# A fused cross-attention and quantised feed-forward kernel: the maximum of h over partitions, the first group's parts, the run-ahead of gelu and p, and the engine of the weights' middle part D

## Chip, cores and metric

One core of a Trainium2 chip runs the whole kernel. The metric is the device time of one execution in microseconds, as a median of several runs. One further execution is recorded by the hardware profiler; all rows of profile below come from such a recording. The engines are called PE (TensorE, the matrix engine), DVE (VectorE), ACT (ScalarE), POOL (GpSimd) and SP (SyncE, which issues most DMAs).

## What is computed

Input x has 2 x 2048 rows of 512. The reference, cut to what matters:

```python
x = x + xattn(layernorm(x), ctx)             # 128 keys per batch, softmax over them
h = layernorm(x)
h = act_qdq(h)                               # 16 bits, one scale: max|h| over the whole tensor
up   = act_qdq(h @ lpbq_dequant(w_up).T)     # 512 -> 1536
gate = act_qdq(h @ lpbq_dequant(w_gate).T)   # 512 -> 1536
sig  = fixed_qdq_u16(sigmoid(gate))
gate = act_qdq(gate * sig)
o    = act_qdq(gate * up)
x = x + o @ lpbq_dequant(w_down).T           # 1536 -> 512
```

`act_qdq` divides by max|x|/32767, rounds, clips and multiplies back; `lpbq_dequant` rounds the weights to 4 bits with a scale for each block of 32. Each `act_qdq` needs the maximum over a whole tensor before the next product can begin, so the program falls into stages.

## The kernel before

The 4,096 rows are 8 groups of 512 (`NG`, `TG`), kept with features on the partitions. A product is made of integers: a 16-bit integer n is split into a = n/4096 rounded, n − 4096a, and 4097a − n, three `parts` in fp32r; a weight is split likewise into H (its high bits), D (weight − H), and a third part made from H and the weight. A "projection" is 12 matmuls of 128x512: 8 into a sum q (parts 0 and 1), then 4 into a sum e (third parts); the value is q·(1 + 1/4096) − e.

The stages, by the profiled execution's span:

- **Prologue, 0 to 177 us.** For each group: `front` (transposes of x, L295; row statistics), `scores` (L314), `turn` (transposes of e into PSUM, then the copy eT on ACT, L419), `attend` (po, L431; x + po, L432), `normalise` (square with row sums on ACT, L449; inverse root on POOL, L284; h on ACT, L460), the maximum of |h| into a column of `hmax` (`abs_max`, L169), and `lift` (transposes of h, L471, copied to hT by ACT, L472). Between them runs `split_weights` for w_gate in four portions of 384 rows, as a generator that is advanced a step at a time: load L175, block maxima L169, scale L181 and L183, integers L185, dequantised L187, transposes L193, copy by ACT L194, then on DVE H (L196), D (L198) and the third part (L201), then the store. The group after the last does its rows one by one.
- **Maximum of h.** `over_partitions` reduces `hmax` to one column on DVE (m_h, L140) and over the partitions on POOL (a_h, L142). `act_scale` makes the scale s_h (L151) and its reciprocal r_h. The integers hi of group 0 are rounded by DVE in four chunks (L542), those of the others in whole, the odd groups by DVE (L549), the even ones by ACT (L551). `split_integers` makes the parts: sa (L235), cast on ACT (L236), then L237 and L238 on DVE.
- **Gate stage, 177 to 455 us.** For each group t and each of three sets k of four weight chunks (n = 3t + k): four projections (L528 for q, L532 for e); g by ACT (L579) and DVE (L580); one step of the preparation of w_up and then w_down (`advance`, again `split_weights`, four portions each); then the maximum of the four (gmax, L169) and a store. PSUM holds three q and three e.
- **Up stage, 455 to 720 us.** 24 tiles in 48 half-tiles c, groups in reverse order: two projections, u by ACT (L726) and DVE (L727), stored to `up_d`; `next_gelu` (three ACT passes over a stored gate tile, L624 to L626) once per tile and once more at c = 1 and c = 13; `integers_of_p` once per tile (L661, DVE), stored to `p_d` (L662); `bound` (|u| on ACT, L669; largest product with p, L670) for a bound of max|o|. In the tile (t, k) = (0, 0), whose half-tiles are c = 42 and 43, the first parts of w_down are loaded (L699), four chunks at the start of it and four at its end.
- **Junction, 720 to 734.5 us.** `fetch_best` takes the best entries of the bound (L676 to L680, giving `row`) and gathers the u and p of those rows by indirect DMA from `up_d` and `p_d` (L685). The maximum of u over the partitions goes through PE: m_u (L765), a transpose of m_u broadcast to 128 columns (L767), and a reduction of the result (L769). ACT rounds u (ui_b, L784), DVE takes the largest products (L786), POOL reduces them over the partitions (L791), DVE makes a_o and a flag; `scale_of_o` (six small DVE operations, L909 to L914) follows, and a branch reads the flag (L926). The branch's body is not run here.
- **Down stage, 734.5 us to the end.** For each 128 rows: oi and its parts (L859 to L866), 36 matmuls (yq L874, ye L882), q scaled by ACT (L887), x added by POOL (L889), e by DVE (L893), store.

Each engine works through its instructions in order. The order of the instructions of one engine comes from a scheduler, which is held in places by `in_order` (an order without a wait). Tiles of a pool are reused after `bufs` further tiles, and wait for the release.

Of the kernel before, what the change touches and what calls it, by code (L numbers as in the profile page):

```python
# [63 lines left out]
P = 128  # L64
# [12 lines left out]
def tile_xattn_ffn(  # L77
# [66 lines left out]

    def act_scale(a, name, unit=None):


        if unit is not None:
            nc.vector.tensor_scalar(a, a, unit, None, ALU.mult)
        s = const.tile([P, 1], F32, name=f"s_{name}")  # L150
        nc.vector.tensor_scalar(s, a, 1.0 / QMAX, TINY, ALU.mult, ALU.max)  # L151
        r = const.tile([P, 1], F32, name=f"r_{name}")
        nc.vector.reciprocal(r, s)
        if unit is not None:
            nc.vector.tensor_scalar(r, r, unit, None, ALU.mult)
        return s, r
# [14 lines left out]
    def split_weights(pool, psum, src, dst, name):  # L171
# [26 lines left out]
        nc.vector.tensor_tensor(ws[:, 1], ws[:, 2], ws[:, 0], ALU.subtract)  # L198
# [58 lines left out]
    with ExitStack() as c0:  # L257

        with ExitStack() as c1:
# [153 lines left out]
            def turn(g, e):  # L413
# [5 lines left out]
                nc.scalar.copy(eT, pe)  # L419
# [86 lines left out]
            lift(NG - 1, hs.pop(NG - 1))  # L506

# [15 lines left out]
        def project(w, parts, q, e):  # L523


            for c in range(ND):
                for s in range(2):
                    nc.tensor.matmul(  # L528
                        q, lhsT=w[:, s, c, :], rhs=parts[:, s, c, :], start=(c + s == 0), stop=(c + s == ND)
                    )  # L530
            for c in range(ND):
                nc.tensor.matmul(e, lhsT=w[:, 2, c, :], rhs=parts[:, 2, c, :], start=(c == 0), stop=(c == ND - 1))  # L532

        with ExitStack() as c2:
            wg = [load_parts(wg_d, f, "wg") for f in range(NF)]
            s_h, r_h = act_scale(*over_partitions(hmax, name="h"), "h")
# [4 lines left out]
            for c in range(ND):  # L541
                nc.vector.tensor_scalar(hi[0][:, c], hT[:, c, :TG], r_h, QMAX, ALU.mult, ALU.min)  # L542
            first = split_integers(wk1, homes[0], hi[0], [ND, TG], "g0", ND)

            table = const.tile([P, 1], F32, name="table")
            nc.scalar.activation(table, unit, AF.Sigmoid)
            for t in range(1, NG):
                if t % 2:
                    nc.vector.tensor_scalar(hi[t], hT[:, :, ts(t, TG)], r_h, QMAX, ALU.mult, ALU.min)  # L549
                else:  # L550
                    nc.scalar.activation(hi[t], hT[:, :, ts(t, TG)], AF.Copy, scale=r_h)  # L551
            hpool.__exit__(None, None, None)
            home1 = tc.tile_pool(name="parts1", bufs=1, side="right")
            homes.append(ctx.enter_context(home1))
            wk2 = c2.enter_context(tc.tile_pool(name="wkb2", bufs=2))
            wpp = c2.enter_context(tc.tile_pool(name="wprep", bufs=1))
# [3 lines left out]
            steps = chain(split_rows(wpp, ps_t, w_up, wu_d, "u"), split_down(wpp, ps_t))  # L560
            groups, wu = {}, []
            for t in range(NG):
# [8 lines left out]
                for k in range(NK):  # L571
                    n = t * NK + k
                    g4 = wk2.tile([P, NQ, TG], F32, tag="g4", name=f"g4_{n}")
                    for i in range(NQ):
                        m = NQ * n + i
                        q = ps_m.tile([P, TG], F32, tag="q", name=f"q_g{m}")
                        e = ps_m.tile([P, TG], F32, tag="e", name=f"e_g{m}")
                        project(wg[NQ * k + i], parts, q, e)
                        nc.scalar.activation(g4[:, i, :], q, AF.Copy, scale=1.0 + 1.0 / BASE)  # L579
                        nc.vector.tensor_tensor_reduce(  # L580
                            g4[:, i, :], g4[:, i, :], e, 1.0, LOWEST, ALU.subtract, ALU.max, gtop[:, m : m + 1]
                        )
                        advance(steps, 1)
# [13 lines left out]
    with ExitStack() as c3:  # L597
# [50 lines left out]
        wd, ready = [], []  # L648
# [9 lines left out]
        def integers_of_p(j):  # L658
            gi, sq = ready[j]
            pi = kept_p[j % NK]  # L660
            nc.vector.scalar_tensor_tensor(pi, gi, k_p, sq, ALU.mult, ALU.mult)  # L661
# [3 lines left out]
            return pi  # L665
# [36 lines left out]
        LAST = len(order) - 1  # L702
        for j, (t, k) in enumerate(order):
# [11 lines left out]
            if j:  # L715
                pi = integers_of_p(j)
            for h in range(2):
# [12 lines left out]
                else:  # L730
                    for i in range(2):
# [6 lines left out]
                        abs_max(umax[:, LAST + 1 + i : LAST + 2 + i], v)  # L738
                stored = nc.sync.dma_start(out=up_d[c], in_=u4[:, both, :])
                if h == 0:  # L740
                    next_gelu()
                if c == 0:
                    pi = integers_of_p(0)

                if c in (1, NH // 4 + 1):
                    next_gelu()
# [10 lines left out]
            if t == 0 and k == 0:  # L757
                load_down(range(NE, NE + NQ), slice(0, 2))
# [5 lines left out]
        m_u = const.tile([P, 1], F32, name="m_u")  # L764
        nc.vector.tensor_reduce(m_u, umax, AX.X, ALU.max)  # L765
        rows = ps_m.tile([P, 2, TG], F32, tag="q", name="rows_u")[:, 0, :P]
        nc.tensor.transpose(rows, m_u.to_broadcast([P, P]), ident)  # L767
        a_u = const.tile([P, 1], F32, name="a_u")
        nc.vector.tensor_reduce(a_u, rows, AX.X, ALU.max)  # L769
# [24 lines left out]
    with ExitStack() as c5:  # L794
# [112 lines left out]
        def scale_of_o(a_o):  # L907

            nc.vector.tensor_scalar(k_o, a_o, 1.0 / QMAX, tiny_o, ALU.mult, ALU.max)  # L909
            nc.vector.reciprocal(k_o, k_o)  # L910
            nc.vector.tensor_tensor(s_o, a_o, s_pu, ALU.mult)
# [4 lines left out]
        uis = {0: up_integers(0)}  # L916
        in_order(rounded[0], *round_up(uis[0], 0, 0, P))
        scale_of_pu()
        a_o = const.tile([P, 1], F32, name="a_o")
# [4 lines left out]
        scale_of_o(a_o)  # L924
        known = nc.values_load(flag[0:1, 0:1], min_val=0, max_val=1)
        with tc.If(known == 0):  # L926
            with tc.tile_pool(name="gen", bufs=1) as gp:
# [37 lines left out]
                a, = over_partitions(omax, name="om")  # L965
                for k in range(NK):
# [6 lines left out]
                scale_of_o(a)  # L973
# [7 lines left out]
        for m in range((last + 1) * NU + 2):  # L981
# [4 lines left out]
            if m <= last * NU + NU - 1:  # L986
# [27 lines left out]
                if m == 0:  # L1014
                    in_order(casts[-1], *round_up(ui, 0, P, P))
# [32 lines left out]
```

## Time and profile before

| | us |
|---|---|
| median of 3 runs (1004.01 to 1007.13) | 1007.1 |
| profiled execution | 1005.54 |
| its span | 1003.7 |
| PE busy in the span | 942.7 (94%) |
| DVE busy | 810.7 (81%) |
| ACT busy | 548.3 (55%) |
| POOL busy | 89.6 (9%) |
| mean granted TensorE clock | 0.976 |

The profile of one execution has a page (busy time per engine; 40 equal slices of the span, each digit the busy share in tenths, PEclk the granted TensorE clock in tenths; DMA queues; the chain of work that ended last; the costliest groups) and a trace that can be asked for stretches and single instructions. In a timeline row come start, duration, engine, line of the kernel, operation, output and inputs with shapes; "[5.06 <-ACT parts_g L236]" says that the engine had been idle for 5.06 us before and what released it; "issue" is idle time in which it waited for nothing that the profile shows. PEld is the weight load of PE, which overlaps the matmuls. Busy time is an average over stages with different limits: what an edit is worth is read from its own stage.

### The profile page before, as it was taken

What the parts mean: (1) busy time and instruction counts of PE and PEld (TensorE: products, weight loads), DVE (VectorE), ACT (ScalarE), POOL (GpSimd) and SP (SyncE); (2) the same over time, 40 slices, a digit from 0 to 9 for tenths busy, and PEclk for the clock granted to TensorE, in tenths of its full rate; (3) what the DMA queues carried; (4) which work ended last, traced back from release to release, by engine and by line L of the source; (5) the groups of instructions that cost most, each with busy time, mean ns of one, the idle gap of its engine ahead of it and who ended that gap; (6) DMA issues with size and microseconds to landing.
All of it is one profiled execution on the core that took longest, in us unless ns stands there. A gap on an engine that the chain in (4) does not pass through costs nothing. (4 is left out here: it accounts for less than half of the span.)

```text
span 1003.7 us, 11683 instructions
## 1 busy us (share of the span) xinstructions
PE 942.7 (94%) x4321; PEld 762.9 (76%) x4321; DVE 810.7 (81%) x1000; ACT 548.3 (55%) x652; POOL 89.6 (9%) x67
## 2 busy tenths in 40 slices
PE   6997884999999999999999999999779999999998
PEld 5765652788888878887788788888557888888886
DVE  4579874999998989645899789887889999888882
ACT  2277786532333223226998998897454445444331
POOL 0101111000000000000000000000011232222221
PEclk9999896999999999999999999999879999999999
DMA  9177652987886666698899798988885676755611
GB/s 345 32 304 283 220 220 79 401 313 303 330 355 248 265 210 210 224 353 328 306 363 375 258 366 328 378 320 328 288 311 215 206 269 222 250 190 160 245 66 43
DMA packets 103596, 263.72 MB, mean 263 GB/s; under 512 B 6064, under 2 KB 46000, under 8 KB 94832
## 3 DMA queue, kind: packets, MB, share of 16 engines
q1 hardware_dynamic: 102496, 259.02, 69.4%
q0 software_dynamic: 512, 2.88, 0.8%
q10 hardware_dynamic: 528, 1.05, 0.3%
q8 instruction: 34, 0.56, 0.2%
q14 instruction: 26, 0.21, 0.1%
HBM read 136.05 MB, written 126.88 MB: 262 GB/s over the span
## 5 line engine op out<-in xcount | busy, mean ns | idle before, releaser
L528 PE MATMUL q_g<-parts_g,wg 128*128 128x512 f32 x768 | 195.0, 394 | 5.1 <-ACT parts_g L236 5.1
L528 PEld LDWEIGHTS q_g<-parts_g,wg 128*128 128x128 f32 x768 | 143.5, 189 | 35.4 <-ACT parts_g L236 5.8
L579 ACT ACTIVATE g<-q_g 128x512 f32<-128x512 f32 x96 | 57.3, 599 | 169.6 <-PE q_g L528 158.9
L528 PE MATMUL q_u<-parts_u,wu 128*128 128x512 f32 x576 | 142.4, 390 | 0.6 <-ACT u L726 0.6
L528 PEld LDWEIGHTS q_u<-parts_u,wu 128*128 128x128 f32 x576 | 108.1, 188 | 23.3 <-ACT u L726 1.0
L874 PE MATMUL yq<-wd,o_parts 128*128 128x512 f32 x512 | 122.1, 391 | 0.0
L874 PEld LDWEIGHTS yq<-wd,o_parts 128*128 128x128 f32 x512 | 96.9, 189 | 20.3
L532 PE MATMUL e_g<-parts_g,wg 128*128 128x512 f32 x384 | 104.0, 392 | 0.1
L580 DVE CUSTOM_DVE_ANT_0 g<-g,e_g 128x512 f32<-128x512 f32 x96 | 64.4, 681 | 37.2 <-PE e_g L532 37.0
L532 PEld LDWEIGHTS e_g<-parts_g,wg 128*128 128x128 f32 x384 | 72.3, 189 | 15.6 <-DVE parts_g L238 0.5
L889 POOL TENSOR_TENSOR qx<-yqs,x 128x512 f32<-128x512 f32 x32 | 63.7, 1991 | 204.3 <-ACT yqs L887 167.9
L874 PE MATMUL yq<-first_wd,o_parts 128*128 128x512 f32 x256 | 65.5, 399 | 13.2 <-ACT o_parts L863 13.2
L887 ACT ACTIVATE yqs<-yq,q_o 128x512 f32<-128x512 f32 x32 | 22.0, 686 | 101.8 <-PE yq L874 101.8
L532 PE MATMUL e_u<-parts_u,wu 128*128 128x512 f32 x288 | 77.1, 390 | 0.0
L866 DVE SCALAR_TENSOR_TENSOR o_parts<-sa,oi 128x1536 fp32r<-128x1536 int16 (+2 forms) x41 | 62.8, 1548 | 15.6 <-PE ye L882 15.6
L863 ACT CAST o_parts<-sa 128x1536 fp32r<-128x1536 int16 (+2 forms) x41 | 48.6, 1189 | 43.9 <-DVE sa L860 43.9
L670 DVE CUSTOM_DVE_ANT_0 ua<-ua,pi 128x1024 f32<-128x1024 f32 x46 | 55.9, 1220 | 16.9 <-ACT ua L669 16.7
L862 DVE SCALAR_TENSOR_TENSOR o_parts<-sa,oi 128x1536 fp32r<-128x1536 int16 (+2 forms) x41 | 59.5, 1451 | 10.9 <-PE yq L874 8.5
L874 PEld LDWEIGHTS yq<-first_wd,o_parts 128*128 128x128 f32 x256 | 48.9, 192 | 24.4 <-ACT o_parts L863 14.2
L727 DVE TENSOR_TENSOR u<-u,e_u 128x1024 f32<-128x1024 f32 x47 | 56.9, 1216 | 12.0 <-ACT u L726 11.9
L661 DVE SCALAR_TENSOR_TENSOR pi<-gi,k_p,sq 128x2048 int16<-128x2048 int16 x24 | 56.4, 2349 | 9.7 <-ACT sq L626 9.7
L882 PE MATMUL ye<-wd,o_parts 128*128 128x512 f32 x256 | 63.2, 389 | 0.0
(185 smaller groups left out, 1553.7 us busy)
## 6 DMA issues: line engine op xcount, KB each, us to landing
gate_d<-g SPq DMA_DIRECT2D x24, 1024.0 KB, 5.5
up_d<-u SPq DMA_DIRECT2D x48, 512.0 KB, 7.2
gt<-gate_d SPq DMA_DIRECT2D x22, 1024.0 KB, 8.6
u<-up_d SPq DMA_DIRECT2D x21, 1024.0 KB, 6.5
parts_d<-parts_g SPq DMA_DIRECT2D x6, 3072.0 KB, 10.9
parts_u<-parts_d SPq DMA_DIRECT2D x6, 3072.0 KB, 13.4
p_d<-pi SPq DMA_DIRECT2D x24, 512.0 KB, 9.7
p<-p_d SPq DMA_DIRECT2D x84, 128.0 KB, 3.3
```

The lines of the kernel that those rows point to most:

```text
L528: nc.tensor.matmul(q, lhsT=w[:, s, c, :], rhs=parts[:, s, c, :], start=(c + s == 0), stop=(c + s == ND))
L532: nc.tensor.matmul(e, lhsT=w[:, 2, c, :], rhs=parts[:, 2, c, :], start=(c == 0), stop=(c == ND - 1))
L579: nc.scalar.activation(g4[:, i, :], q, AF.Copy, scale=1.0 + 1.0 / BASE)
L580: nc.vector.tensor_tensor_reduce(g4[:, i, :], g4[:, i, :], e, 1.0, LOWEST, ALU.subtract, ALU.max, gtop[:, m : m + 1])
L661: nc.vector.scalar_tensor_tensor(pi, gi, k_p, sq, ALU.mult, ALU.mult)
L670: nc.vector.tensor_tensor_reduce(ua, ua, pi, 1.0, 0.0, ALU.mult, ALU.max, pumax[:, c : c + 1])
L727: less = nc.vector.tensor_tensor(u4[:, both, :], u4[:, both, :], e, ALU.subtract)
L862: made.append(nc.vector.scalar_tensor_tensor(parts[1][:, c], sa[:, c], -BASE, oi[:, c], ALU.mult, ALU.add))
L866: return nc.vector.scalar_tensor_tensor(parts[2][:, c], sa[:, c], BASE + 1.0, oi[:, c], ALU.mult, ALU.subtract)
L874: nc.tensor.matmul(q, lhsT=parts[s][:, f, :], rhs=wd[f][:, s, :], start=(f + s == 0), stop=(f + s == NF))
L882: nc.tensor.matmul(e, lhsT=parts[2][:, f, :], rhs=wd[f][:, 2, :], start=(f == 0), stop=(f == NF - 1))
L889: nc.gpsimd.tensor_tensor(qx, qs, x1[:, m % NU, :], ALU.add)
```

## The change

Six edits:

1. **Maximum of h.** `over_partitions_by_pe` does for h what was written out for u; a_h is made at the end of the prologue, inside its pools.
2. **eT of the last group** is copied by DVE instead of ACT.
3. **First group's parts by chunks.** `first_integers`: chunk 0 is rounded by DVE, chunks 1 to 3 by ACT; the parts 0 and 1 of each chunk follow at once, the third parts last. In n = 0, the q of the first two projections comes ahead of their e. The integers of groups 1 to 7 are made during n = 0, one by DVE and one by ACT behind each of its projections (only DVE behind the last). Preparation starts after n = 0 and goes two steps per projection in n = 1, one afterwards. The second buffer of g4 and the second home of the parts are opened after n = 0.
4. **D on POOL.** The subtraction that makes D, in all twelve portions, moves from DVE to GpSimd; the third part, on DVE, now waits for it.
5. **Up stage.** One more gelu at each of c = 1, 13, 19, 31, and one more p at c = 17 and 27; p is made behind u's evacuation of the first half-tile instead of ahead of it. The second set of w_down loads is issued ahead of the store of u in c = 43 instead of behind the tile.
6. **Scale of o.** `scale_of_o` is cut in two: `factor_of_o` (k_o, two operations) stays ahead of the branch, the four others go behind the first sums of the down stage.

```diff
+    def over_partitions_by_pe(pool, tag, shape, stats, name):
+        m = const.tile([P, 1], F32, name=f"m_{name}")
+        nc.vector.tensor_reduce(m, stats, AX.X, ALU.max)
+        rows = pool.tile(shape, F32, tag=tag, name=f"rows_{name}")
+        rows = rows[:, 0, :P] if len(shape) == 3 else rows[:, :P]
+        nc.tensor.transpose(rows, m.to_broadcast([P, P]), ident)
+        a = const.tile([P, 1], F32, name=f"a_{name}")
+        nc.vector.tensor_reduce(a, rows, AX.X, ALU.max)
+        return a
     def act_scale(a, name, unit=None):
...
         yield
-        nc.vector.tensor_tensor(ws[:, 1], ws[:, 2], ws[:, 0], ALU.subtract)
+        nc.gpsimd.tensor_tensor(ws[:, 1], ws[:, 2], ws[:, 0], ALU.subtract)
         yield
...
                 eT = wk2.tile([P, NJ, P], F32, tag="eT", name=f"eT_{g}")
-                nc.scalar.copy(eT, pe)
+                if g < NG - 1:
+                    nc.scalar.copy(eT, pe)
+                else:
+                    nc.vector.tensor_copy(eT, pe)
                 return eT
...
             lift(NG - 1, hs.pop(NG - 1))
+            a_h = over_partitions_by_pe(ps_o, "o", [P, D], hmax, "h")
...
+            project_q(w, parts, q)
+            project_e(w, parts, e)
+        def project_q(w, parts, q):
             for c in range(ND):
...
                     )
+        def project_e(w, parts, e):
             for c in range(ND):
...
+        def first_integers(pool_a, r_h):
+            n = hi[0]
+            a = pool_a.tile([P, ND, TG], I16, tag="sa", name="sa_g0")
+            parts = homes[0].tile([P, 3, ND, TG], F32R, tag="parts", name="parts_g0")
+            rounded, casts, made = [], [], []
+            for c in range(ND):
+                if c == 0:
+                    made.append(nc.vector.tensor_scalar(n[:, c], hT[:, c, :TG], r_h, QMAX, ALU.mult, ALU.min))
+                else:
+                    rounded.append(nc.scalar.activation(n[:, c], hT[:, c, :TG], AF.Copy, scale=r_h))
+                made.append(nc.vector.tensor_scalar(a[:, c], n[:, c], 1.0 / BASE, None, ALU.mult))
+                casts.append(nc.scalar.copy(parts[:, 0, c], a[:, c]))
+                made.append(
+                    nc.vector.scalar_tensor_tensor(parts[:, 1, c], a[:, c], -BASE, n[:, c], ALU.mult, ALU.add)
+                )
+                if c:
+                    in_order(rounded[c - 1], casts[c - 1])
+            for c in range(ND):
+                made.append(
+                    nc.vector.scalar_tensor_tensor(
+                        parts[:, 2, c], a[:, c], BASE + 1.0, n[:, c], ALU.mult, ALU.subtract
+                    )
+                )
+            in_order(*made)
+            return parts, casts[-1]
+        def integers_of_h(t):
+            if t % 2:
+                return nc.vector.tensor_scalar(hi[t], hT[:, :, ts(t, TG)], r_h, QMAX, ALU.mult, ALU.min)
+            return nc.scalar.activation(hi[t], hT[:, :, ts(t, TG)], AF.Copy, scale=r_h)
         with ExitStack() as c2:
             wg = [load_parts(wg_d, f, "wg") for f in range(NF)]
-            s_h, r_h = act_scale(*over_partitions(hmax, name="h"), "h")
+            s_h, r_h = act_scale(a_h, "h")
...
             wk1 = c2.enter_context(tc.tile_pool(name="wkb1", bufs=1))
-            for c in range(ND):
-                nc.vector.tensor_scalar(hi[0][:, c], hT[:, c, :TG], r_h, QMAX, ALU.mult, ALU.min)
-            first = split_integers(wk1, homes[0], hi[0], [ND, TG], "g0", ND)
+            first, last_cast = first_integers(wk1, r_h)
             table = const.tile([P, 1], F32, name="table")
-            nc.scalar.activation(table, unit, AF.Sigmoid)
-            for t in range(1, NG):
-                if t % 2:
-                    nc.vector.tensor_scalar(hi[t], hT[:, :, ts(t, TG)], r_h, QMAX, ALU.mult, ALU.min)
-                else:
-                    nc.scalar.activation(hi[t], hT[:, :, ts(t, TG)], AF.Copy, scale=r_h)
-            hpool.__exit__(None, None, None)
-            home1 = tc.tile_pool(name="parts1", bufs=1, side="right")
-            homes.append(ctx.enter_context(home1))
-            wk2 = c2.enter_context(tc.tile_pool(name="wkb2", bufs=2))
-            wpp = c2.enter_context(tc.tile_pool(name="wprep", bufs=1))
+            in_order(last_cast, nc.scalar.activation(table, unit, AF.Sigmoid))
+            g4_homes = [c2.enter_context(tc.tile_pool(name="g4_0", bufs=1))]
             ps_m = c2.enter_context(tc.tile_pool(name="ps_m", bufs=3, space=PSUM))
...
-            steps = chain(split_rows(wpp, ps_t, w_up, wu_d, "u"), split_down(wpp, ps_t))
-            groups, wu = {}, []
+            steps, groups, wu = None, {}, []
             for t in range(NG):
...
                     n = t * NK + k
-                    g4 = wk2.tile([P, NQ, TG], F32, tag="g4", name=f"g4_{n}")
+                    g4 = g4_homes[n % 2].tile([P, NQ, TG], F32, tag="g4", name=f"g4_{n}")
+                    sums = [
+                        [ps_m.tile([P, TG], F32, tag=tag, name=f"{tag}_g{NQ * n + i}") for tag in "qe"]
+                        for i in range(2)
+                    ]
+                    if n == 0:
+                        for i in range(2):
+                            project_q(wg[i], parts, sums[i][0])
                     for i in range(NQ):
                         m = NQ * n + i
-                        q = ps_m.tile([P, TG], F32, tag="q", name=f"q_g{m}")
-                        e = ps_m.tile([P, TG], F32, tag="e", name=f"e_g{m}")
-                        project(wg[NQ * k + i], parts, q, e)
-                        nc.scalar.activation(g4[:, i, :], q, AF.Copy, scale=1.0 + 1.0 / BASE)
-                        nc.vector.tensor_tensor_reduce(
+                        if i < 2:
+                            q, e = sums[i]
+                        else:
+                            q, e = (ps_m.tile([P, TG], F32, tag=tag, name=f"{tag}_g{m}") for tag in "qe")
+                        if n == 0 and i < 2:
+                            project_e(wg[i], parts, e)
+                        else:
+                            project(wg[NQ * k + i], parts, q, e)
+                        evacuated = nc.scalar.activation(g4[:, i, :], q, AF.Copy, scale=1.0 + 1.0 / BASE)
+                        subtracted = nc.vector.tensor_tensor_reduce(
                             g4[:, i, :], g4[:, i, :], e, 1.0, LOWEST, ALU.subtract, ALU.max, gtop[:, m : m + 1]
                         )
-                        advance(steps, 1)
+                        if n == 0:
+                            in_order(subtracted, integers_of_h(2 * i + 1))
+                            if i < NQ - 1:
+                                in_order(evacuated, integers_of_h(2 * i + 2))
+                        if n:
+                            advance(steps, 2 if n == 1 else 1)
+                    if n == 0:
+                        hpool.__exit__(None, None, None)
+                        homes.append(ctx.enter_context(tc.tile_pool(name="parts1", bufs=1, side="right")))
+                        g4_homes.append(c2.enter_context(tc.tile_pool(name="g4_1", bufs=1)))
+                        wpp = c2.enter_context(tc.tile_pool(name="wprep", bufs=1))
+                        steps = chain(split_rows(wpp, ps_t, w_up, wu_d, "u"), split_down(wpp, ps_t))
                     abs_max(gmax[:, n : n + 1], g4, AX.XY)
...
-        wd, ready = [], []
+        wd, ready, made_p = [], [], []
...
-        def integers_of_p(j):
+        def next_p():
+            j = len(made_p)
+            if j == len(order):
+                return
             gi, sq = ready[j]
             pi = kept_p[j % NK]
+            made_p.append(pi)
             nc.vector.scalar_tensor_tensor(pi, gi, k_p, sq, ALU.mult, ALU.mult)
...
             )
-            return pi
...
         LAST = len(order) - 1
+        more_gelu = (1, NH // 4 + 1, 3 * NH // 8 + 1, 5 * NH // 8 + 1)
+        more_p = (NH // 3 + 1, NH // 2 + 3)
         for j, (t, k) in enumerate(order):
...
             u4 = tiles_u[j % NK]
-            if j:
-                pi = integers_of_p(j)
             for h in range(2):
...
                         abs_max(umax[:, LAST + 1 + i : LAST + 2 + i], v)
+                if t == 0 and k == 0 and h == 1:
+                    load_down(range(NE, NE + NQ), slice(0, 2))
                 stored = nc.sync.dma_start(out=up_d[c], in_=u4[:, both, :])
-                if h == 0:
+                if h == 0 or c in more_gelu:
                     next_gelu()
-                if c == 0:
-                    pi = integers_of_p(0)
-                if c in (1, NH // 4 + 1):
-                    next_gelu()
+                if h == 0 or c in more_p:
+                    next_p()
+                pi = kept_p[j % NK]
                 if c + 3 < NH:
...
                 abs_max(umax[:, j : j + 1], u4[:, :2, :], AX.XY)
-            if t == 0 and k == 0:
-                load_down(range(NE, NE + NQ), slice(0, 2))
...
-        m_u = const.tile([P, 1], F32, name="m_u")
-        nc.vector.tensor_reduce(m_u, umax, AX.X, ALU.max)
-        rows = ps_m.tile([P, 2, TG], F32, tag="q", name="rows_u")[:, 0, :P]
-        nc.tensor.transpose(rows, m_u.to_broadcast([P, P]), ident)
-        a_u = const.tile([P, 1], F32, name="a_u")
-        nc.vector.tensor_reduce(a_u, rows, AX.X, ALU.max)
+        a_u = over_partitions_by_pe(ps_m, "q", [P, 2, TG], umax, "u")
...
-        def scale_of_o(a_o):
+        def factor_of_o():
...
             nc.vector.reciprocal(k_o, k_o)
+        def scale_of_o():
             nc.vector.tensor_tensor(s_o, a_o, s_pu, ALU.mult)
...
         uis = {0: up_integers(0)}
+        a_o = const.tile([P, 1], F32, name="a_o")
         in_order(rounded[0], *round_up(uis[0], 0, 0, P))
         scale_of_pu()
-        a_o = const.tile([P, 1], F32, name="a_o")
         nc.vector.tensor_reduce(a_o, top[:, 0:3], AX.X, ALU.max)
...
             nc.vector.scalar_tensor_tensor(flag, top[:, 3:4], floor, a_o, ALU.max, ALU.is_le)
-        scale_of_o(a_o)
+        factor_of_o()
         known = nc.values_load(flag[0:1, 0:1], min_val=0, max_val=1)
...
                 a, = over_partitions(omax, name="om")
+                nc.vector.tensor_copy(a_o, a)
                 for k in range(NK):
...
                 scale_of_pu()
-                scale_of_o(a)
+                factor_of_o()
...
                 if m == 0:
+                    scale_of_o()
                     in_order(casts[-1], *round_up(ui, 0, P, P))
```

## The prediction

> **What bounds the kernel now.** I read the 40 slices first: where is TensorE (PE) not busy, and at which clock?
>
> ```profile
> PE   6997884999999999999999999999779999999998
> DVE  4579874999998989645899789887889999888882
> PEclk9999896999999999999999999999879999999999
> ```
>
> PE is full except in slices 5 to 7 (125 to 175 us) and 28 to 30 (700 to 750 us), and there its clock falls too. VectorE (DVE) is nearly full in slices 7 to 15. Next, busy time and granted clock of stretches (PE, PEld, DVE, ACT, POOL, then clock, DMA share, GB/s):
>
> ```profile
> 150.00:175.00 25.00, 11.79 (x40) 6.65 (x40) 10.82 (x35) 17.31 (x31) 3.56 (x6) 0.69 0.20 80
> 175.00:200.00 25.00, 22.92 (x92) 17.88 (x93) 23.85 (x40) 14.46 (x17) 0.00 (x0) 0.90 1.01 400
> 300.00:350.00 50.00, 50.00 (x234) 41.27 (x233) 44.84 (x62) 15.31 (x24) 0.00 (x0) 1.00 0.71 263
> 725.00:750.00 25.00, 15.48 (x57) 12.63 (x58) 19.86 (x44) 12.36 (x19) 1.95 (x2) 0.71 0.90 323
> ```
>
> At 300 to 350 PE has no gap: 24 matmuls take 5.44 us, so the 3,456 of the three products need 783.4 us at 0.2267 each. None of them is removed. Time can come only from the two holes, and be lost only by making DVE late enough to open new ones. The chain of waits covers only 765 to the end, all PE, and says nothing of the holes; so the timeline of each hole came next.
>
> **First hole, 146 to 184 us: maximum of h and first parts.** Lines: start, duration, engine, operation, idle before.
>
> ```profile
> 153.17 0.57 ACT L419 COPY eT<-pe 128x512 f32<-128x512 f32 x1
> 153.79 4.63 PE L431 MATMUL po<-vsb,eT 128*128 128x512 f32 x5 [4.77 <-ACT eT L419]
> ...
> 169.80 0.17 DVE L140 TENSOR_REDUCE m_h<-hmax 128x1 f32<-128x11 f32 x1
> ...
> 173.59 0.38 POOL L142 PARTITION_ALL_REDUCE a_h<-m_h  x1 [5.65 <-issue]
> 174.00 0.15 DVE L151 TENSOR_SCALAR s_h<-a_h 128x1 f32<-128x1 f32 x1 [4.04 <-POOL a_h L142]
> ...
> 177.02 0.80 PE L528 MATMUL q_g<-parts_g,wg 128*128 128x512 f32 x1 [5.06 <-ACT parts_g L236]
> ```
>
> m_h ends at 169.97, yet GpSimd (POOL) starts a_h at 173.59: 5.65 us after its last work, "issue", with nothing awaited. From m_h to s_h it is 4.03. The maximum of u already goes the new way, at the end of the up stage:
>
> ```profile
> 721.50 0.18 DVE L765 TENSOR_REDUCE m_u<-umax 128x1 f32<-128x26 f32 x1
> ...
> 721.83 0.29 PE L767 MATMUL rows_u<-ident,m_u 128*128 128x128 f32 x1 [1.88 <-DVE m_u L765]
> 722.16 0.29 DVE L769 TENSOR_REDUCE a_u<-rows_u 128x1 f32<-128x128 f32 x1 [0.48 <-PE rows_u L767]
> ```
>
> m_u's end (721.68) to a_u's end (722.45) is 0.77. A rule speaks against this: the Trainium skill, "GPSIMD Engine Reference", section 4.1, puts a reduction along partitions on GpSimd. By the rule this part is a loss; by the rows it wins 4.03 − 0.77 ≈ 3.2. I take the rows. The same page (section 2.1) has about 6 us for the first call of a freshly loaded GpSimd routine, which fits the 5.65, so it would come back at the next such call, a_g at 458: about +1.4 there by my count from its queue. That is covered, because PE has u's projections and ScalarE (ACT) can evacuate them.
>
> The eT copy of the last group goes from ACT to DVE. On ACT it stood behind four L449 squares, and PE idled 4.77 and DVE 3.13 before it. On DVE it can end near 151.5, so the last po follow some 2 us earlier. The new order also puts hmax of group 6 (2.29 at 157.88) behind the last xt, and both last lifts before the transposed row. Walking the new orders with the old durations, m_h ends near 167.0 instead of 169.97: 3.0. Ends: 0 if the queue of ACT binds anyway, 4.5 if all the idle goes. Sum at s_h: 6.2.
>
> **Ramp.** First matmul came 3.02 after s_h (four L542, 1.67 together, before the first sa), and the first 24 took 7.16 instead of 5.44. Now one DVE chunk (0.43), then sa, cast, parts follow by chunk, and ACT rounds the others; q of two projections goes ahead of any e, so the third part is wanted later. First matmul near +2.2, and most of the 1.7 goes. The hi of groups 1 to 7 (2.49 on DVE, 2.00 on ACT each) is spread over n=0, where preparation steps are now none (two per projection in n=1 make up). I take −2.0; ends −2.8 and 0.
>
> **D on GpSimd (12 times).** The rows, of D on DVE and of POOL's nearest work (min/median/max ns):
>
> ```profile
> L198 DVE TENSOR_TENSOR wsp_u<-wsp_u x4: 1751/1752/1753, 215.1 to 292.4; 128x1536 f32<-128x1536 f32 x4
> L889 POOL TENSOR_TENSOR qx<-yqs,x x32: 1281/2087/2686, 745.6 to 998.1; 128x512 f32<-128x512 f32 x32
> ```
>
> By the row D is at most 3 × 1.28 = 3.84. The same section 4.1 advises VectorE for elementwise work, and section 3.1 has 4.50 us for 2,048 elements, so 3.4. I take 3.6. The third part needs D and follows on DVE, which works in order: where nothing stands between, DVE waits 3.6, not 1.75. And the two engines block each other:
>
> ```profile
> 808.12 1.75 DVE L866 SCALAR_TENSOR_TENSOR o_parts<-sa,oi 128x1536 fp32r<-128x1536 int16 x1
> ...
> 813.91 2.04 POOL L889 TENSOR_TENSOR qx<-yqs,x 128x512 f32<-128x512 f32 x1 [7.99 <-DMA out<-qx]
> ...
> 814.71 2.85 DVE L866 SCALAR_TENSOR_TENSOR o_parts<-sa,oi 128x1536 fp32r<-128x1536 int16 x1
> ```
>
> The same L866 takes 1.75 alone and 2.85 from 814.71, ending 1.6 after POOL's. The skill's "SBUF — State Buffer" (Who interferes with whom) calls it an exclusive lock on two shared ports: the second blocks for the whole first. Here that means up to 3.6 for a DVE operation with two SBUF inputs (L237, L185, L187).
>
> - Prologue, four D: by the new DVE order one has the third part directly behind (+2.1), one six microseconds of work between (−1.75), two little (+0.5, +0.3). DVE sets the pace of groups with preparation (about 20 us, DVE working all of it), so this lands on PE: +1.0 (−2 to +3).
> - Gate stage, eight D: about six waits or blocks near 3 us, 17 of DVE lost for 14 saved. PE has three buffers: g (L580) ran 0.15 to 5.5 behind its matmuls, and PE stalls beyond some 6.5. I count +0.7 (−1 to +4). The 1.84 PE stall at 374 (transposes behind a late w_d) may go or move.
>
> **Up stage.** Gelus and p run further ahead (two more gelus, two more p, store of p earlier). Before, PE stalled once per extra gelu by 0.3 to 0.6; two more: +0.5 (0 to +1.5).
>
> **Second hole, 716 to 734.5 us.**
>
> ```profile
> 715.98 0.16 DVE L680 SCALAR_TENSOR_TENSOR row<-where,lane 128x1 uint32<-128x1 uint32 x1
> ...
> 720.47 1.08 POOL L685 DMA_INDIRECT best<-up_d,row  x1 [261.86 <-DMA up_d<-u]
> ...
> 729.62 1.23 DVE L786 CUSTOM_DVE_ANT_0 product_b<-ui_b,best 128x1024 f32<-128x1024 int16 x1 [3.12 <-DMA best<-p_d,row]
> ...
> 734.52 0.80 PE L874 MATMUL yq<-first_wd,o_parts 128*128 128x512 f32 x1 [12.39 <-ACT o_parts L863]
> ```
>
> The row is known at 716.14, but the gather starts at 720.47, waiting for up_d: the queue carried w_down (L699 at 705.55), then p_d, up_d, p_d, up_d. Now the last p_d go out before those loads, and the loads one half-tile earlier. Then the gather can start near 716.4; its data come 6.7 and 7.6 later, at 723 and 725. Next late is the chain of ACT ui_b (from 722.93) and DVE products: the third ends near 727.6 instead of 730.85, so 3.2. Four tiny DVE operations (0.15 each) leave the path to the branch: 0.2. Sum −3.4; ends 0 (DMA still busy) and −4.
>
> **Sum**, against the profiled execution's 1005.54: −6.2 −2.0 +1.0 +0.7 +0.5 −3.4 = −9.4, so 996.1. The median of the runs shown is 1.6 above it: **997**.
>
> **Rivals.** A measurement here tells about 0.3% (3 us).
> - A, as above, 0.55: 992 to 1000.
> - B, the order at 150 gives nothing (ACT's squares and identities bind before as after: 17.3 of 25 busy) and the ramp half: −3.2 −1.0 −3.4 +2.2 = −5.4, so 1001. For it: ACT sits in every link of that tail. Against: DVE and PE both idled for eT alone. 0.17.
> - C, the gather meets a queue still draining (DMA share 0.72 there) and D costs some more: −3.2 −2.0 +4 = −1, so 1006. 0.12.
> - D, slower: DVE in the gate stage. It is at 24 of 25 us until 300. If a POOL D takes 5 us because DVE blocks it too (L889 reaches 2.7 for 1.28, twice), H to third part costs 3.3 net each time: +13 over four in the prologue, and in the gate stage a lag already at 3 us passes 6.5, eight times about 1 to 2 us on PE. +24 −11 = +13 at worst; half of it, about +6: 1012. It decides from D ≈ 5 us. For it: nearly full DVE. Against: many neighbours read PSUM, and L893 (PSUM and SBUF) never slowed beside POOL. 0.16.
>
> Range 988 to 1007: A and B with the ends of their terms, most of C. Chances: faster 0.72 (A, B), same 0.12 (C), slower 0.16 (D).
>
> **What would show it.** Right: no POOL operation between m_h and s_h, 0.8 between them; first gate matmul near 169 to 171; the L198 work on POOL at 3.4 to 3.9; the gather within 1 us of the row; about 11 us between the last up matmul and the first yq, 14.6 before. Wrong: D above 5 us, groups of the prologue longer than 20 us, new PE idle before q_g at 200 to 410 with an L580 as releaser, or the gather still behind up_d.

## The result, and the profile after

The changed kernel takes 1005.91 us (median of 12 runs), the kernel before 1006.59 (12 runs beside it): ratio 0.9994, interval 0.9982 to 1.0005. No difference can be told, where 997 was forecast. The changed kernel's profiled execution has a span of 1006.9 us, the one before 1003.7; single executions of one kernel differ by as much (the profiled one was the slowest of the changed kernel's twelve, 1008.64 us), so differences of time below come from medians, and profiles say where a difference sits.

The 40 slices of the changed kernel:

```profile
PE   6988886999999999999999999999879999999998
DVE  4468877898889898644989888988799998788882
PEclk9999997999999999999999999999989999999999
```

In the seventh slice, the first hole, PE stands at 6 instead of 4 and the clock at 7 instead of 6. The fall of PE at the junction (slices 29 and 30) is still there. What the digits hide is in the stretches (PE, PEld, DVE, ACT, POOL, clock, DMA share, GB/s):

```profile
225.00:250.00 25.00, 23.32 (x109) 19.07 (x108) 21.71 (x28) 8.15 (x12) 0.12 (x1) 1.00 0.70 283
275.00:300.00 25.00, 23.12 (x100) 18.51 (x99) 20.75 (x27) 9.24 (x14) 6.39 (x2) 0.93 0.72 262
```

Before, PE was busy for 24.95 and 25.00 us of these. A digit of 9 can hide a loss of 1.9 in 25, and five windows in a row, 225 to 350, lose 0.8 to 1.9 each.

The timeline of the first hole after:

```profile
168.64 0.16 DVE L148 TENSOR_REDUCE m_h<-hmax 128x1 f32<-128x11 f32 x1
...
169.62 0.15 DVE L162 TENSOR_SCALAR s_h<-a_h 128x1 f32<-128x1 f32 x1
...
171.99 5.52 PE L547 MATMUL q_g<-parts_g,wg 128*128 128x512 f32 x16 [2.73 <-ACT parts_g L567]
```

From m_h's end to s_h it is 0.82 (4.03 before), and the first matmul of the gate stage comes at 171.99 instead of 177.02. Five microseconds were won by then. They are lost here (timeline rows of the gate stage; in the changed kernel's numbering L209 is D, L207 H, L212 the third part, L246 and L249 are sa and a part of h, L204 the transposes of the weights that L198 has dequantised):

```profile
220.64 3.51 POOL L209 TENSOR_TENSOR wsp_u<-wsp_u 128x1536 f32<-128x1536 f32 x1 [53.85 <-DVE wsp_u L207]
221.08 3.61 DVE L246 TENSOR_SCALAR sa_g<-hi 128x2048 int16<-128x2048 int16 x1
...
230.88 1.20 PE L553 MATMUL e_g<-parts_g,wg 128*128 128x512 f32 x4 [1.68 <-DVE gtop L636]
...
266.72 1.06 PE L204 MATMUL wt_u<-ident,w_u 128*128 128x128 f32 x8 [1.65 <-issue]
...
280.34 1.76 DVE L212 SCALAR_TENSOR_TENSOR wsp_u<-wsp_u 128x1536 f32<-128x1536 f32 x1 [3.06 <-POOL wsp_u L209]
```

sa takes 3.61, not its usual 0.69: it started while D was running and ended 0.54 after it. DVE waits 3.06 for D at 277. What DVE loses reaches PE in two ways: at 231 the sum e has no free PSUM buffer because g (L636) is late, and at 267 PE stands in its own order before transposes whose weights DVE has not made yet ("issue", since the profile sees no semaphore; L198 ends at 266.6). PE idles 8.0 us so in the gate stage (1.68, 1.65, 1.87, 0.77, 1.75, 0.30); before it was 1.84. Three of these are new waits of PE between 200 and 410 us with g as releaser, which the prediction had named as a sign of being wrong (it had them ahead of q; they are ahead of e). And behind the stall of 1.87 the granted clock was 0.51 for 3.4 us (284.8 to 288.2; it is the 0.93 of the second row above), which is another 1.7 us.

The junction and the start of the down stage:

```profile
719.36 0.16 DVE L751 SCALAR_TENSOR_TENSOR row<-where,lane 128x1 uint32<-128x1 uint32 x1
...
721.11 1.19 POOL L756 DMA_INDIRECT best<-up_d,row  x1 [254.14 <-DVE u L800]
...
735.83 1.65 PE L940 MATMUL yq<-first_wd,o_parts 128*128 128x512 f32 x3 [8.93 <-ACT o_parts L929]
...
764.49 2.50 PE L940 MATMUL yq<-first_wd,o_parts 128*128 128x512 f32 x8 [2.10 <-ACT o_parts L929]
```

The gather no longer waits for a DMA, and the last up matmul (ends 724.73) is 11.1 us ahead of the first yq, not 14.6. The gather still starts 1.6 us behind the row, where the prediction had at most 1. And at 764 PE now waits 2.10, where the longest wait of this stage was 0.56 before: ACT stands in L903 (ui) behind reloads of u, the second of which is there 24.5 us behind the first yq, 23.2 before.

The whole, by stretches of the spans. The last column is the run with D back on DVE, told below:

| stretch | before | after | forecast | after − before | without D on POOL − before |
|---|---|---|---|---|---|
| start to s_h | 174.00 | 169.62 | −5.2 | −4.4 | −9.8 |
| s_h to third projection | 10.41 | 9.54 | −2.0 | −0.9 | −0.4 |
| to first up matmul | 271.21 | 279.97 | +0.7 | **+8.8** | +1.1 |
| to last up matmul's end | 264.33 | 265.60 | +0.5 | +1.3 | +1.2 |
| to first yq | 14.57 | 11.10 | −3.4 | −3.5 | −3.5 |
| to the end | 269.18 | 271.07 | 0 | +1.9 | +0.9 |
| span | 1003.7 | 1006.9 | −9.4 | +3.2 | −10.4 |

### The profile page after: what moved, and what is told of

It reads as the page before. It is cut to its first block, busy times and chain, and to the rows that moved or that the text cites. A ratio compares the mean times of both kernels' runs of the same rounds, so it can differ in the third digit from the quotient of the medians.

```text
span 1006.9 us, 11697 instructions
## 1 busy us (share of the span) xinstructions
PE 944.6 (94%) x4322; PEld 764.8 (76%) x4322; DVE 798.6 (79%) x987; ACT 547.9 (54%) x654; POOL 129.5 (13%) x78
## 5 line engine op out<-in xcount | busy, mean ns | idle before, releaser
L636 DVE CUSTOM_DVE_ANT_0 g<-g,e_g 128x512 f32<-128x512 f32 x96 | 63.9, 677 | 38.3 <-PE e_g L553 37.4
L932 DVE SCALAR_TENSOR_TENSOR o_parts<-sa,oi 128x1536 fp32r<-128x1536 int16 (+2 forms) x41 | 60.1, 1483 | 19.1 <-PE ye L948 19.1
L928 DVE SCALAR_TENSOR_TENSOR o_parts<-sa,oi 128x1536 fp32r<-128x1536 int16 (+2 forms) x41 | 59.5, 1451 | 12.5 <-PE yq L940 10.6
L741 DVE CUSTOM_DVE_ANT_0 ua<-ua,pi 128x1024 f32<-128x1024 f32 x46 | 56.0, 1219 | 12.8 <-ACT ua L740 12.7
L553 PEld LDWEIGHTS e_u<-parts_u,wu 128*128 128x128 f32 x288 | 54.0, 188 | 11.9 <-DVE u L800 0.7
```

The source lines that it names most:

```text
L636: subtracted = nc.vector.tensor_tensor_reduce(g4[:, i, :], g4[:, i, :], e, 1.0, LOWEST, ALU.subtract, ALU.max, gtop[:, m : m + 1])
L741: nc.vector.tensor_tensor_reduce(ua, ua, pi, 1.0, 0.0, ALU.mult, ALU.max, pumax[:, c : c + 1])
L928: made.append(nc.vector.scalar_tensor_tensor(parts[1][:, c], sa[:, c], -BASE, oi[:, c], ALU.mult, ALU.add))
L932: return nc.vector.scalar_tensor_tensor(parts[2][:, c], sa[:, c], BASE + 1.0, oi[:, c], ALU.mult, ALU.subtract)
```

## Experiments

Two theories stood at the start. **T1**: the gains came, and D on GpSimd gave them back. **T2**: the shifted preparation (none in n = 0, twice the steps in n = 1) gave them back, whichever engine makes D.

**D on DVE again**, all else as changed:

```diff
-        nc.gpsimd.tensor_tensor(ws[:, 1], ws[:, 2], ws[:, 0], ALU.subtract)
+        nc.vector.tensor_tensor(ws[:, 1], ws[:, 2], ws[:, 0], ALU.subtract)
```

> The changed kernel with one edit undone: D of the weights on DVE again, all else as changed. Theory T1 (the gains came, and D on GpSimd gave them back: its lock on DVE operations with two SBUF inputs and the third part's wait make g late, and PE stalls at 231, 267, 284, 307 and 345 us): those five stalls (7.7 us together) shrink to at most 2, and the time is 6 to 10 us below the changed kernel's, about 997 to 999. Rival T2 (the loss comes from the preparation of w_up that starts after n=0 and goes two steps at a time in n=1, whichever engine makes D): the stalls stay, and the time stays within 2 us of 1006.

Measured: 995.04 us, ratio 0.989 (0.9872 to 0.9907), 10.9 below the changed kernel. In the gate stage PE waits for more than 1 us twice, and once for 0.20:

```profile
251.20 1.19 PE L553 MATMUL e_g<-parts_g,wg 128*128 128x512 f32 x4 [1.30 <-DVE gtop L636]
...
284.23 2.12 PE L547 MATMUL q_g<-parts_g,wg 128*128 128x512 f32 x8 [1.18 <-ACT g L635]
```

T1 holds: one line of the change costs 10.9 us, and the rest brings 11.1. In the profiles the stretch from the third projection to the first up matmul is 7.7 shorter (272.3 for 280.0): 5.3 less idle time of PE and 1.7 for the half clock at 285, which this run does not have. The other 0.7 the profiles don't resolve.

**One preparation step per projection in n = 1**, D on GpSimd:

```diff
-                            advance(steps, 2 if n == 1 else 1)
+                            advance(steps, 1)
```

> The changed kernel with one preparation step per projection in n=1 instead of two. T2: the first stall at 231 us goes and the time falls by 2 us or more. T1: within 2 us of the changed kernel, 1006, with the stalls only moved to other projections.

Measured: 1004.27, ratio 0.998 (0.9969 to 0.999). The stall stays (228.82, 1.71), others move. T2 is worth about 1.6 us, hardly more than the spread of the runs tells.

**Only D moved, in the kernel before:**

```diff
-        nc.vector.tensor_tensor(ws[:, 1], ws[:, 2], ws[:, 0], ALU.subtract)
+        nc.gpsimd.tensor_tensor(ws[:, 1], ws[:, 2], ws[:, 0], ALU.subtract)
```

> The kernel before with only D moved to GpSimd. T1: 6 to 10 us slower than before, 1013 to 1017, with new PE idle in the gate stage between 200 and 410 us behind L580. T2: no more than 2 us slower.

Measured: 1009.92, ratio 1.0036 (1.0025 to 1.0047): 3.8 slower, less than T1 said. The stretches tell why. Its way from the first gate matmul to the first up matmul is 289.1 us (173.87 to 462.93) against 278.6 before, 10.5 lost; but m_h ends 3.1 earlier and the gap before the first yq is 11 us too. The scheduler had put other work of DVE and ACT in another order, with no edit there. A part tried alone is not the part alone: what the order brings is in it.

**Where D hurts.** GpSimd for w_gate alone (the prologue), or for w_up and w_down alone (the gate stage; the same line with `!=`):

```diff
+        (nc.gpsimd if name[0] == "g" else nc.vector).tensor_tensor(ws[:, 1], ws[:, 2], ws[:, 0], ALU.subtract)
```

> The changed kernel with D on GpSimd for w_gate alone (the four portions of the prologue); the eight of the gate stage on DVE. It splits the 10.9 us between 995.0 (no D on GpSimd) and 1005.9 (all twelve). From the first gate matmul of the profiles (166.46 without, 171.98 with) the prologue's share would be 5.5, less about 1.7 that may be the clock: 999 to 1001. If the whole loss is the gate stage's (the stalls there): 995 to 997.

> The changed kernel with D on GpSimd for w_up and w_down alone, w_gate's on DVE. 995.0 plus the 8.2 us that are left of the loss after the prologue's 2.7: 1002 to 1004, with the PE stalls of 1 to 2 us between 200 and 410. If the portions hurt only together with the prologue's: 998 or less.

Measured: 997.75 (ratio 0.9912, 0.9899 to 0.9924) and 1003.4 (0.9963, 0.9952 to 0.9975). So the prologue costs 2.7 us and the gate stage 8.4; the sum, 11.1, agrees with the 10.9 of both. How much of the prologue's part is waiting stays open: in the profiles s_h comes 2.8 later than with all D on DVE, but of the time up to 160 us there are also 10.2 us at half clock instead of 6.8.

**Lock or wait?** In the gate stage an extra GpSimd subtraction of the same size that nobody waits for, with all D on DVE:

```diff
+        if name[0] != "g":
+            nc.gpsimd.tensor_tensor(w, w, w, ALU.subtract)
```

> All D on DVE, and in the gate stage an added GpSimd subtraction of the same size per portion, in place on a weight tile that is no longer needed: nothing waits for its result, it only shares the ports. If the lock makes the gate stage's part of the loss (about 5 to 7 us): 999 to 1002, with DVE operations 2 to 3 us longer beside it. If the third part's wait for D makes it: at most 2 us above 995. What the added work costs by the reuse of its tile is in it too.

Measured: 1000.52, ratio 0.9941 (0.9927 to 0.9956): 5.5 above 995.04. Here the lock falls on H (L209 in this kernel):

```profile
213.05 3.05 POOL L208 TENSOR_TENSOR w_u<-w_u 128x1536 f32<-128x1536 f32 x1 [53.12 <-PE wt_u L204]
213.57 3.34 DVE L209 TENSOR_SCALAR wsp_u<-wsp_u 128x1536 uint32<-128x1536 uint32 x1
```

H usually takes 0.96. Seven of the eight are longer, by 1.2 to 2.4, 12.8 us together. So 5.5 us are lost though no engine waits for a result; that the weight tile is free for its next load only behind the added operation is in it too.

The opposite trial, D of w_up and w_down on GpSimd in three pieces, so that each hold is short (w_gate's stays on DVE):

```diff
+            for b in range(3):
+                nc.gpsimd.tensor_tensor(ws[:, 1, b], ws[:, 2, b], ws[:, 0, b], ALU.subtract)
```

> As the run with D on GpSimd for w_up and w_down alone, but each D in three pieces of 512, so that the ports are held for about 1.2 us at a time. If what costs is one long hold in front of a DVE operation: 2 us or more below that run. If it is the wait of the third part for the whole D, which stays near 3.6: within 1 us of it.

Measured: 1001.34 (ratio 0.9956, 0.9938 to 0.9975), 2.1 below the undivided 1003.4, which the spread of the runs hardly tells. Blocked DVE operations lose 1.6 us in all instead of 10.7, but the third part then waits 16.9 in all instead of 8.2, as in this row:

```profile
273.77 1.76 DVE L216 SCALAR_TENSOR_TENSOR wsp_u<-wsp_u 128x1536 f32<-128x1536 f32 x1 [3.30 <-POOL wsp_u L213]
```

Lock and wait are two faces of one thing: while GpSimd spends 3.5 us on D, DVE either stands in a blocked operation or waits for the result. In both runs DVE loses 18 to 19 us to save 14 (8 × 1.75), and PE idles 8.5 us with the pieces, 8.0 without.

**The third part later:**

```diff
+        if name[0] != "g":
+            yield
+            yield
```

> The changed kernel, D on GpSimd, but for w_up and w_down the third part comes two projections (5.4 us) later, so DVE never waits for D there; DVE operations with two SBUF inputs can still be blocked. If the wait for D is the cost (8.3 us of DVE idle at the third part in the gate stage): 4 us or more below 1006. If the lock is (four DVE operations of the gate stage longer by 2.4 to 3.0 each): at most 2 us below, and such long operations are still there.

Measured: 1014.08, ratio 1.0077 (1.0064 to 1.009). It doesn't answer the question. Waits for D sum to 16.0, prologue included, 14.0 in the changed kernel: the scheduler put the third part behind D again. From the first gate matmul to the first up matmul it took 280.4 us instead of 287.1; but the preparation ended 30 us later, the first gate tiles of the up stage were loaded at 470 instead of 445 and 457, and PE stalled there once for 13.4 us. One thing it does show: in the gate stage DVE lost 15.6 us to D here, yet the stage took no longer than with D on DVE (280.1).

The price on PE doesn't follow DVE's sum, then. After the 14 us saved are taken off, DVE was 4.9 us worse off with D on GpSimd and 8.4 were lost; 12.8 worse off with the extra operation, where nothing is saved, and 5.5 were lost; 1.6 worse off with the third part later, and the gate stage lost next to nothing. What is left as the cause is when the losses fall, against the lag of g and the transposes; no run moved a single loss to show it.

**Maximum of h on GpSimd**, D on DVE:

```diff
-            a_h = over_partitions_by_pe(ps_o, "o", [P, D], hmax, "h")
+            (a_h,) = over_partitions(hmax, name="h")
```

> The changed kernel with D on DVE and the maximum of h over partitions on GpSimd as before. The rows before gave 3.2 us to the way through TensorE (4.03 from m_h to s_h against 0.77): 998 to 999, s_h about 4 us behind m_h. If the tail of the prologue hides it: 995 to 996.

Measured: 998.48, ratio 0.9917 (0.9893 to 0.9941): 3.4 slower than with TensorE, from six runs that spread over 8.6 us; the rows below put s_h 3.73 behind m_h's end, 0.97 in the run with TensorE, a difference of 2.8.

```profile
163.18 0.17 DVE L140 TENSOR_REDUCE m_h<-hmax 128x1 f32<-128x11 f32 x1
...
167.08 0.15 DVE L162 TENSOR_SCALAR s_h<-a_h 128x1 f32<-128x1 f32 x1 [3.73 <-POOL a_h L142]
```

**eT of the last group on ACT**, D on DVE:

```diff
-                if g < NG - 1:
-                    nc.scalar.copy(eT, pe)
-                else:
-                    nc.vector.tensor_copy(eT, pe)
+                nc.scalar.copy(eT, pe)
```

> The changed kernel with D on DVE and eT of the last group on ACT as before. The prediction gave 3.0 us to the copy and the order that comes with it: 997 to 998, PE idle before the last po again near 4.8. If the order came from elsewhere: within 1 us of 995.

Measured: 1003.01, ratio 0.9958 (0.9942 to 0.9974): 8.0 slower, against 3.0 expected.

```profile
152.16 0.58 ACT L430 COPY eT<-pe 128x512 f32<-128x512 f32 x1
152.79 5.35 PE L442 MATMUL po<-vsb,eT 128*128 128x512 f32 x6 [4.77 <-ACT eT L430]
```

With DVE, eT starts at 148.29, 3.9 earlier, and m_h ends at 163.21 instead of 168.96: 5.75. Of both, 0.8 was there ahead of the copy (an earlier po at 131.97 instead of 132.76), so 3.1 and 5.0 are the copy's and its order's. That the other 1.9 come with the order of hmax of group 6, which stands ahead of the last xt here (156.88) and behind them there, is read from the rows and was not tried alone. What is left to 8.0 is the ramp in part (first matmul 2.96 behind s_h instead of 2.28); the rest the profiles don't resolve.

**Edits 1 and 2 alone**, in the kernel before (lines as in the change):

```diff
+            a_h = over_partitions_by_pe(ps_o, "o", [P, D], hmax, "h")
...
+                    nc.vector.tensor_copy(eT, pe)
```

> The kernel before with edits 1 and 2 alone (maximum of h through TensorE, eT of the last group on DVE). Sums of the runs so far, 3.4 for the maximum and 5 to 8 for eT: 996 to 998. By the prediction's own terms (3.2 and 3.0): 1000 to 1001.

Measured: 994.66, ratio 0.9879 (0.9855 to 0.9903). They alone bring all that the change without D brings; edits 3, 5 and 6 together bring nothing that can be measured (995.04). But not all of these 11.9 us is the two edits' own work: in this run's profile the gap before the first yq is 11.4 us instead of 14.6, with no edit there (see below).

**Edit 5 undone**, D on DVE:

```diff
-                if h == 0 or c in more_gelu:
-                    next_gelu()
-                if h == 0 or c in more_p:
-                    next_p()
+                if h == 0:
+                    next_gelu()
+                if c == 0:
+                    next_p()
+                if c in more_gelu:
+                    next_gelu()
...
+            if t == 0 and k == 0:
+                load_down(range(NE, NE + NQ), slice(0, 2))
```

(with `more_gelu = (1, NH // 4 + 1)`, and p at the head of each tile)

> The changed kernel with D on DVE and edit 5 undone (gelus, p and the second set of w_down loads as in the kernel before). If edit 5 frees the gather of the best entries, as the prediction had it: the gather again waits for up_d, the gap from the last up matmul to the first yq is 14 to 15 us instead of 11.1. Of the 3.5 us lost there some 1.5 to 2 come back in the down stage, whose stall at 752 us (2.5) shrinks: 996 to 998 against 995.0. If the gap shrank for another reason: 11 to 12 us, and the time within 1 us of 995.

Measured: 993.8, ratio 0.988 (0.9861 to 0.99). The gap is 11.1 us without the edit too, and the up stage is 1.4 shorter (264.2 against 265.6). What had kept the gather waiting in the kernel before is in its timeline at half-tile 43:

```profile
697.54 7.92 SPq L739 DMA_DIRECT2D up_d<-u  x2
...
701.49 2.15 ACT L726 ACTIVATE u<-q_u 128x1024 f32<-128x1024 f32 x2
```

ACT took that half-tile's u only behind three gelu passes, at 701.49; the store of u waited, SP stood in it, and the loads of w_down behind it were issued at 705.55, to run into the last stores. With edit 5 undone but the rest kept, the same code goes:

```profile
688.46 1.03 ACT L800 ACTIVATE u<-q_u 128x1024 f32<-128x1024 f32 x1 [0.38 <-PE q_u L547]
688.83 2.27 SPq L813 DMA_DIRECT2D up_d<-u  x2
```

u first, the loads at 691.20. It is an accident of order, absent from three kernels that have edit 5's code as before: this one, edits 1 and 2 alone, D alone. In these three the gather starts 0.9 us behind the row.

## Why the prediction was wrong

**The failed step is "D on GpSimd": the price on PE.** It had +1.0 for the prologue and +0.7 (−1 to +4) for the gate stage; measured are 2.7 and 8.4, 11.1 instead of 1.7. The duration was right (3.6 taken, 3.43 to 3.52 measured), and so was DVE's balance in the gate stage: 17 lost for 14 saved, 18.9 measured. What failed is the step from there to PE. "PE stalls beyond some 6.5" was used as if losses were spread evenly. They come in lumps: a blocked operation (sa 3.61 us, L249 4.66 to 5.27), with the third part and the block maxima (1.74 each) next in line ahead of g, onto a lag that had reached 5.5 before. A second door was seen but not counted: transposes of weights, in PE's order, stall PE as soon as DVE is late with them (1.65, 1.75, 0.30), with no buffer between. And a term was missing: a stall of PE can bring half clock behind it, here 1.7 us.

**The rest of the sum came true by luck.** Without D the forecast's own terms make −11.1 (−6.2 −2.0 +0.5 −3.4), and the run without D is 11.1 below the kernel before. But eT brought more than forecast, the ramp nothing that can be measured, and the junction's part is not owed to the edit that was to bring it, as told below. (Added exactly, the forecast is 997.7, not 997.)

**Rivals.** C had the time (1006), D the mechanism: DVE in the gate stage. D's point of decision, a D of 5 us, was false. It decided at 3.5.

**Maximum of h**: right, 3.2 forecast, 3.4 measured in the medians and 2.8 in the rows. The rule of the Trainium skill that was weighed against it ("GPSIMD Engine Reference", 4.1) loses here. A delay at a_g did come back, as forecast: it starts 4.9 us behind m_g in the changed kernel, 0.1 before and in the run with a_h on GpSimd. That is more than the +1.4 of the forecast, and PE's waits in the up stage did not grow by it (3.6 us together in the run with D on DVE, 4.3 in the one with a_h on GpSimd).

**eT and order**: right mechanism, size 3.0 against 8.0 in the median and 5.0 to 5.75 at m_h. The gain of 3.1 to 3.9 at eT was put at 2, and the order of hmax comes on top, as far as the rows show; the upper end, 4.5, was too low.

**Ramp**: −2.0 forecast, −0.9 and −0.4 in the profiles, nothing in the medians. The first matmul came 2.37 and 2.28 us behind s_h instead of 3.02, as forecast; "most of the 1.7" did not come. First the row before, then that of the run with D on DVE (stretches of 2 us):

```profile
178.00:180.00 2.00, 2.00 (x6) 1.39 (x5) 2.00 (x6) 1.99 (x3) 0.00 (x0) 0.52 1.00 415
```

```profile
168.00:170.00 2.00, 2.00 (x6) 1.56 (x5) 1.97 (x4) 1.87 (x3) 0.00 (x0) 0.50 0.98 406
```

PE is busy throughout with six matmuls in 2 us, at a granted clock of 0.5, in both kernels. The first parts were not what mainly stretched the first 24 matmuls; the clock after the hole was, until about 180.0 before and 171 here. From the first matmul to the 25th it is 7.39 us before (the 7.16 of the prediction ends at the 24th), 1.95 more than at full speed, and 2.9 us at half clock make 1.5 of it. In the two kernels after, 7.17 and 7.76, the 3.4 and 4.7 us at half clock make the whole loss: the 0.5 that is left before was won, and the clock took it back in one of the two. The Trainium skill, "TensorE: Matmul & The Clock Gate" (Part 1), says that what is issued in the first 3.4 us or so after idling runs at half clock. By that rule earlier parts only move the slow stretch; the traces agree roughly (2.9 us before, 3.4 and 4.7 after).

**Junction**: −3.4 forecast, −3.5 in the gap. The number was right by luck and its cause wrong: edit 5 doesn't make it. Whether some of it comes back in the down stage stays open: the changed kernel's profile has +1.9 there (the wait of 2.10 and 3.4 us at half clock behind it), the run with D on DVE +0.9, but in the nine other variants of the changed kernel, with gaps of 11.1 to 11.4, this stretch takes 269.2 to 269.6 us, 269.2 before.

**Up stage**: +0.5 forecast, +1.2 to +1.3 in the profiles; undoing edit 5 gives 1.2 in the median, within the intervals of the two runs.

The best kernel that ran has edits 1, 2, 3 and 6, at 993.8 us. It can't be told from edits 1 and 2 alone (994.66).

## What to carry to other kernels

Moving an operation off a nearly full engine paid nothing here, because the receiving engine blocked the first or was waited for at once. Count the time that the first engine stands, blocked or waiting, against what it saves; then ask how the lumps meet the buffers in front of the bounding engine, since the sum alone didn't tell the price here. Work of the bounding engine that stands in its order and needs the late one's result (here transposes between matmuls) has no buffer at all. And where a scheduler decides, a part that moves the time may do it through an order nobody edited, so look at the same stretch in several variants before a gain is put down to an edit.

## What the runs showed of the hardware

- While GpSimd ran D, some DVE operations that began beside it were held till about its end, small ones too: nmx (L334), 128x4 elements with two SBUF inputs, took 2.30 us instead of 0.16; sa with one SBUF input 3.61 instead of 0.69. Others were not: g (L636, which reads PSUM) took its usual 0.68 twice beside D at 326.5, and a reduction over SBUF (L180, at 104.02) its usual 2.28.
- It works the other way too: in the run with three pieces, L253 had begun on DVE ahead of a piece of D, and that piece took 3.34 us (243.99) instead of 1.29.
- GpSimd took 3.43 to 3.52 us for the subtraction of 128x1536 f32, DVE 1.75, ratio 2.0.
- A stall of PE of 1.87 us in the changed kernel, and one of 1.84 in the run with D on GpSimd in the gate stage alone, had 3.4 us at a granted clock of 0.5 behind them. Two of 2.06 in the run with pieces had none, so the length of the stall alone doesn't decide it.
- The clock's dips in the prologue differ from profile to profile: between 50 and 75 us it was 0.93 in the profile before and 1.00 in the run with D on DVE, and the same work behind it (a po at 133.77) came 1.8 us earlier there. So some 1.8 of the −9.8 in the table above is the clock.
